# A four-layer graph network on one core: layer 0's sums turned, two of its quarters side by side, and the start of layer 1

## The chip, the core and the metric

The kernel runs on one core of one Trainium2 chip. The metric is the device time of one execution in microseconds (us), median of the runs shown. TensorE (PE) multiplies matrices, VectorE (DVE) and ScalarE (ACT) work on elements, GpSimd (POOL) takes powers, casts and issues the converting loads, and SyncE (SP) issues the other transfers. Matrix products land in eight PSUM banks, each 128 partitions by 512 float32.

## What is computed

4096 nodes with 64 features each (`x`) pass through four layers; `adj` is a 4096 x 4096 matrix of zeros and ones. Each layer normalizes `x`, takes the positive part `h`, and adds a graph operation to `x`:

```python
# layer 0: of each row's ones, the last 100 count, weighted by halves from the end
rank = jnp.cumsum(mask, axis=1); deg = rank[:, -1:]; k = jnp.minimum(deg, 100.0)
w = mask * jnp.where(rank - (deg - k) > 0, 0.5 ** (k - (rank - (deg - k))), 0.0)
x = x + w @ (h @ weight) + bias
# layer 1: attention between linked nodes; q, k and h come from small linear steps
att = adj * sigmoid((2 + 2 * (qm @ k.T)) / att_scale + att_bias)
support = att @ h;  x = x + support / norm(support)
# layer 2: two gated steps, each with adj @ (...);  layer 3: adj @ (66 columns), then an output map
```

## The kernel before

**Tiles.** `adj` stands in memory turned (`adjT`, sources by targets, float32). The targets are cut into four quarters q of 1024 and the sources into 32 blocks b of 128, so there are 128 blocks (q, b) of 128 x 1024. All 128 stay in SBUF as one byte per element, in the tiles `A` (two blocks in one tile). Nothing is loaded twice for the layers: layers 1 to 3 read `A`.

**Layer 0** (`stream0`, called once for each quarter, blocks from 31 down to 0). 113 blocks are loaded by a DMA that POOL issues and that converts float32 to bytes (`dma` at L1025). One such load waits until the load eight before it has landed (`after=loads[-8:-7]`). The other 15 (`staged`) are loaded as float32 by SP, cast by POOL (L1210) and tested on DVE (L1187), which looks for values other than 0 and 1. The byte pairs are read as float16, two elements in one number. For each half c of a block, PE adds a product with the triangular matrix `tri` (`ftri` in the profile) into a PSUM bank, which then holds each place's count of later ones in a coded form. `weigh` on ACT (L1233) or DVE (L1235) turns the count into the weight 2^-count, in 128 x 512 pieces. Then a product with `upd` (`fupd`) turns the bank into the start of the next block. So tri, weigh, upd, tri is a chain through all the blocks of a quarter, one for each half. `add` multiplies the weights as stationary operand (four 128 x 128 pieces) with `S0`, the layer's input in two float16 parts of 64 columns, into `sums`.

**After a quarter** `post0` reduces the sums on DVE (two reductions at L990), turns them with four transposes (L1038), multiplies with `w0` and adds to `X[q]`. `pre1` then computes that quarter's share of layer 1: `S1`, the keys `kT` and the queries, with four powers on POOL (`root`, L997), four turns and three linear steps on PE, and a number of DVE and ACT steps. The queries go out to memory and back in another order (`qs`).

**Layer 1** (`stream1`) goes by quarters, and in each by 16 pairs of blocks. A pair takes two scores on PE (four products of a 64 x 64 corner of the array each), a sigmoid on ACT (L1008, `fatt_mul`), a product with `A` on DVE (L968) and two adds on PE. Pair i needs `kT[i // 4]`. Scores take two neighbouring PSUM banks out of banks 0 to 3, and the accumulator takes two out of 4 to 7.

**What sets the order.** `Plan.order` writes each engine's instructions in one fixed order, made from planned costs, priorities and free PSUM banks and SBUF tiles. On the chip each engine goes through its list in order. So an instruction that waits holds all behind it. On POOL the powers, the casts and the issue of loads share one list. Layer 1's scores have a lower priority than all of layer 0. The 113 blocks not tested in layer 0 are tested later, in layers 1 and 2. `load_x` and `load_consts` bring the four quarters of `x` and the weights in between the first blocks (`gate`, L1683).

In the scheduled order of before, three scores stand ahead of the last `tri` product of quarter 3, and the rest behind it.

Of the kernel before, what the change touches and what calls it, by code (L numbers as in the profile page):

```python
# [38 lines left out]
def general_kernel(ctx: ExitStack, tc: tile.TileContext, t: dict, out: bass.AP):  # L39
# [11 lines left out]
    adjT = t["adjT"]  # L51
    N = adjT.shape[0]
    NB = N // P
# [163 lines left out]
    def aggregate(m, lhs, weigh, descending, evac, post):  # L217
# [8 lines left out]
        for h in range(NH):  # L226
# [16 lines left out]
            for i, pair in enumerate(pairs):  # L243
                a = adjp.tile([P, 2, HN], F32, tag="a", name="a")
                nc.sync.dma_start(a, adjT[pair * 2 * P:(pair + 1) * 2 * P, h * HN:(h + 1) * HN]
                                  .rearrange("(j p) n -> p j n", p=P))
                for s in range(NCH // 2):
                    rhs = weigh(h, i, pair, s, a)
                    if behind is not None:
                        accumulate(*behind)  # L250
                    behind = (i, pair, s, rhs)
                if h > 0 and i == 1:
                    post(h - 1)
# [380 lines left out]
class Plan:  # L634
# [7 lines left out]
    TABLE = 1.28  # L642
    RATE = 0.42e6
    LAND = 2.0

    def __init__(self, nsb, limits, anywhere):
        self.ops = []
        self.nsb = nsb
        self.limits = limits
        self.anywhere = anywhere  # L650
        self.clock = 0.0

# [43 lines left out]
    def find(self, b):  # L696
# [20 lines left out]
        if self.psn.get(b.kind, 0) + b.units > self.limits.get(b.kind, 8):  # L717
            return math.inf, None
        places = range(0, 4, 2) if b.units == 2 else range(8) if b.kind in self.anywhere else range(4, 8)
        if b.kind != "nw" and self.psn.get("single", 0) >= 3:  # L720
# [180 lines left out]
def fast_kernel(ctx: ExitStack, tc: tile.TileContext, t: dict, out: bass.AP, flag: bass.AP):  # L901
    nc = tc.nc
    adjT = t["adjT"]
    N = adjT.shape[0]
    NB = N // P
# [8 lines left out]

    plan = Plan(NSB, {"cnt": 2, "sum": 2, "sc": 4, "acc": 3, "acc2": 3, "acc3": 6, "nw": 4,
                      "w": (24, 16), "g": (5, 6), "stage": (5, 8), "qd": (4, 0), "mx": (4, 0)}, ("sum", "acc3"))

# [229 lines left out]

    loads = []

# [27 lines left out]
    def staged(q, b):  # L1177
        n = q * NB + NB - 1 - b
        return n > 8 and n % 8 == 1

# [12 lines left out]
    def later_test(b, q, after, cost):  # L1193
        s = sb(4, "stage")
        dma(s, View(None, lambda: adjT[b * P:(b + 1) * P, q * 2 * CW:(q + 1) * 2 * CW]), P * 2 * CW * 5, 8.0, after=after)
        return test(b, q, s, 9.0, cost)


    def stream0(q, behind):
        cnt = [bank("cnt") for _ in range(2)]  # L1200
        sums = [bank("sum") for _ in range(2)]
        for b in range(NB)[::-1]:
            a = a8(q, b)
            src = View(None, lambda b=b: adjT[b * P:(b + 1) * P, q * 2 * CW:(q + 1) * 2 * CW])
            if b in behind:
                behind[b](loads[-1:], (q, b + 1))
            if staged(q, b):
                s = sb(4, "stage")
                dma(s, src, P * 2 * CW * 5, 1.0, after=loads[-2:-1])
                plan.op({"POOL": 1.4}, lambda e, a=a, s=s: G_.tensor_copy(a.get().bitcast(U8), s.get(), saturate=False),  # L1210
                        (s,), (a,), 1.0)
                test(b, q, s, 1.9, {"DVE": 1.58})
            else:
                loads.append(dma(a.bits(U8), src, P * 2 * CW * 4, 0.9 if len(loads) < 2 else 1.0, "POOL", after=loads[-8:-7]))
            wts = []
            for c in (0, 1):
                pairs = slice(c * CW // 2, (c + 1) * CW // 2)

                def count(e, c=c, a=a, pairs=pairs, b=b, wt=tri):
                    mm(cnt[c].get()[:, :CW // 2], wt, a.get().bitcast(F16)[:, pairs], False, b == 0)  # L1220

                if b == NB - 1:
                    plan.op({"PE": 0.12}, lambda e, c=c: mm(cnt[c].get()[:, :CW // 2], mean16, half16, True, False),
                            (triv,), (cnt[c],), 1.0, "full")
                plan.op({"PE": 0.112}, count, (a, triv), (cnt[c],), 1.0, "full")
                wt = sb(1, "w").bits(I16)
                wts.append(wt)

                def weigh(e, c=c, wt=wt):
                    o = wt.get().rearrange("p (n k) -> p n k", k=2)  # L1230
                    s = cnt[c].get()[:, :CW // 2].bitcast(I8).rearrange("p (n k) -> p n k", k=4)[:, :, :2]
                    if e == "ACT":
                        S_.activation(o, s, AF.Relu, scale=-128.0)  # L1233
                    else:
                        V.tensor_scalar(o, s, -128.0, 0.0, op0=ALU.mult, op1=ALU.max)  # L1235
                plan.op({"ACT": 0.6, "DVE": 0.69}, weigh, (cnt[c],), (wt,), 0.5)
                if b:
                    plan.op({"PE": 0.112}, lambda e, count=count: count(e, wt=upd), (a, triv), (cnt[c],), 1.0, "full")
            for c in (0, 1):
                def add(e, b=b, c=c, wt=wts[c]):  # L1240
                    s = S0[b // QB].get()[:, b % QB]
                    o = sums[c].get().rearrange("p (k n) -> p k n", k=4)
                    for d in range(4):
                        mm(o[:, d, :].rearrange("p (k d) -> p k d", d=D), wt.get()[:, d * P:(d + 1) * P].bitcast(BF16), s,
                           b == NB - 1 and d == 0, b == 0)
                plan.op({"PE": 0.24}, add, (wts[c], S0[b // QB]), (sums[c],), 2.0, "full")
        return sums

    def post0(q, sums, prio):
        g = nodes("agg")  # L1250
        for c in range(2):
            red(g.part(c)[:, c * CB:(c + 1) * CB, :], sums[c].re("p (b k d) -> p b d k", k=2, d=D), CW, prio)
        fm = sb(2, "aggT")
        copy(fm, turn4(flat(g), prio), prio=prio, scale=W0 / HALF)
        tt(X[q], X[q], blocks(linear4(fm, w("w0"), prio)), ALU.add, prio=prio)
        pre1(q, prio)
# [77 lines left out]
    ends = {}  # L1334
    scores = []

    def stream1(q):
        qd = []
        for c in range(2):
# [5 lines left out]
            qd.append(v)  # L1345
        acc = [bank("acc") for _ in range(2)]
        for i in range(NB // 2):
            gs = []
            for c in range(2):
                ps = bank("sc", 2)  # L1350

                def score(e, i=i, c=c, ps=ps):
                    kb = kT[i // 4].get()[:, (i % 4) * P:(i % 4 + 1) * P]
                    o = ps.get().rearrange("p (j n) -> p j n", j=2)
                    for h in range(2):
                        for j in range(2):
                            half = slice(j * D, (j + 1) * D)
                            mm(o[h * D:(h + 1) * D, j, :], kb[half, h * D:(h + 1) * D], qd[c].get()[half, :])
                scores.append(plan.op({"PE": 0.856}, score, (kT[i // 4], qd[c]), (ps,), 3.0, "corner", after=scores[-1:]))
                g = sb(4, "g")  # L1360
                fn(g, ps, AF.Sigmoid, 1280, 1.0, "sig", View(attv.buf, lambda: att_add), View(attv.buf, lambda: att_mul))
                g3 = g.re("p (j n) -> p j n", j=2)
                m = g.re("p (k n) -> p k n", n=P)
                tt(m, m, A[q][i].bits(U8).re("p j (k c n) -> p c (j k) n", c=2, n=P)[:, c], ALU.mult, 2 * CW, 1.0)
                gs.append(g3)
            for j in range(2):
                def add(e, i=i, j=j, gs=gs):
                    b = 2 * i + j
                    s = S1[b // QB].get()[:, b % QB, :]
                    for r in range(2):  # L1370
                        half = slice(r * D, (r + 1) * D)
                        for c in range(2):
                            mm(acc[r].get()[c * D:(c + 1) * D, :], s[half, :], gs[c].get()[half, j, :], b == 0, b == NB - 1)
                ends[1, q, i] = plan.op({"PE": 0.856}, add, (*gs, S1[(2 * i) // QB]), tuple(acc), 3.1, "corner")
        return acc

    def post1(q, acc, prio):
        a = sb(2, "a")
        fn(a, acc[0], AF.Copy, prio=prio)
        tt(a, a, acc[1], ALU.add, prio=prio)  # L1380
        sup = blocks(turn4(a, prio))
# [309 lines left out]
    def load_consts(after, behind):  # L1691
        gate(Wv, lambda: W[:1, :1], behind)
        dma(Wv, View(None, lambda: t["consts"][:, :L.at["scales"].stop]), P * L.at["scales"].stop * 4, 0.1, after=after)
        for q in range(NQ):
# [4 lines left out]
    load_x(3)  # L1699
    behind = {NB - 2: lambda *a: load_x(2, *a), NB - 5: lambda *a: load_x(1, *a), NB - 9: lambda *a: load_x(0, *a),  # L1700
              NB - 13: load_consts}
    sums = {}
    for q in range(NQ):
        sums[q] = stream0(q, behind if q == 0 else {})
        post0(q, sums[q], 0.9 if q < NQ - 1 else 0.4)
    acc = {}
# [46 lines left out]
    return plan  # L1753


def pack_consts(given):
# [84 lines left out]
```

## Time and profile before

| what | value |
|---|---|
| median of the runs, lowest, highest | 689.85, 689.84, 690.35 us |
| the profiled execution, and its span | 691.17, 689.3 us |
| granted TensorE clock, mean | 0.976 |
| busy PE, DVE, ACT, POOL | 622.3, 548.6, 450.6, 167.9 us |
| last `tri` product | 202.2 us after the span's start |
| converting loads | 113 of 128 KB landed each, 9.9 us to landing (median) |
| float32 block loads by SP | 128 of 512 KB, 5.7 us to landing (median) |
| in `x_pm` loads, weights | 4 of 256 KB, 1 of 456.5 KB |

"Busy" PE includes the time in which a product runs through the array with the next one already started, so it can stand near 100% with room left. The rate in GB/s counts the bytes that land: of a converting load these are a quarter of what is read. Times in the views are microseconds from the span's start, and "x" is the number of instructions.

### The profile page before, as it was taken

The page shows a single profiled execution, that of the slowest core. Times are in us where ns is not written, and L with a number is a line of the kernel's source. Part 1 is how long each engine was busy: PE and PEld are TensorE (multiplying, and loading weights), DVE is VectorE, ACT ScalarE, POOL GpSimd, SP SyncE. Part 2 cuts the span into 40 slices and gives each one's busy share as a digit, 9 for nine tenths or more (in the row PEclk, how much of TensorE's full clock was granted, in tenths as well). Part 3 has the DMA queues.
Part 4 walks back from the last instruction along what each step waited for, and adds up shares of the span by engine and source line. Part 5 has one row for each costly group of instructions (what it writes and reads, how often), then busy time and mean ns, then how long its engine had stood idle before and what let it go on. Part 6 is the DMA issues. An engine that isn't in the chain of part 4 may idle for free.

```text
span 689.3 us, 14988 instructions
## 1 busy us (share of the span) xinstructions
PE 622.3 (90%) x6060; PEld 355.2 (52%) x6060; DVE 548.6 (80%) x1030; ACT 450.6 (65%) x680; POOL 167.9 (24%) x188
## 2 busy tenths in 40 slices
PE   4788889899999999999999999999999999999950
PEld 2666668678764443333333333344444444599950
DVE  5675776776768899998987799887988988985585
ACT  3464757577666666676665567645987698984463
POOL 6535564574422200200110010011000022202141
PEclk9899999999999999999999999999999999999995
DMA  9999989989902233422322231369689978420001
GB/s 99 181 251 106 95 66 147 178 73 157 125 17 62 77 93 97 120 62 93 108 57 97 92 112 62 123 220 390 202 264 352 342 250 260 154 63 2 3 31 36
DMA packets 39934, 91.64 MB, mean 133 GB/s; under 512 B 4656, under 2 KB 19632, under 8 KB 39856
## 3 DMA queue, kind: packets, MB, share of 16 engines
q1 hardware_dynamic: 23584, 75.78, 33.1%
q0 software_dynamic: 16272, 14.82, 24.2%
q8 instruction: 49, 0.80, 0.5%
q14 instruction: 29, 0.24, 0.1%
HBM read 130.82 MB, written 2.10 MB: 193 GB/s over the span
## 4 chain that ended last, share of the span: by engine, by line
PE 63%; DVE 16%; DMA 8%; ACT 6%; issue 3%; POOL 3%; SPq 0%; POOLq 0%; ACTq 0%; DVEq 0%
PE p L1029 61%; DVE m L968 4%; DMA A<-in_adjT 3%; ACT m L1008 3%; PE p L1038 3%; DMA m<-in_adjT 3%; DVE m L1235 2%; DVE m L985 2%; POOL s L997 2%; DMA m<-in_x_pm 2%; ACT m L1233 2%; DVE s L990 2%; DVE junk L1187 2%; POOL A L1025 1%; DVE s L968 1%
## 5 line engine op out<-in xcount | busy, mean ns | idle before, releaser
L1029 PE MATMUL p<-m,m 64*64 64x512 f32 (+1 forms) x3012 | 337.8, 476 | 8.5 <-ACT m L1008 3.7
L997 POOL TENSOR_TENSOR s<-s,powers 128x8 f32<-128x8 f32 (+1 forms) x45 | 89.3, 1992 | 461.4 <-DVE s L979 199.4
L1008 ACT ACTIVATE m<-p,fatt_add,fatt_mul 128x1024 f32<-128x1024 f32 x128 | 149.6, 1201 | 77.2 <-PE p L1029 63.6
L1029 PEld LDWEIGHTS <-m 128*128 128x128 bf16 (+1 forms) x2048 | 134.0, 105 | 75.5 <-issue 22.0
L968 DVE TENSOR_TENSOR m<-m,A 128x1024 f32<-128x1024 f32 x128 | 152.8, 1221 | 19.8 <-ACT m L1008 19.4
L1029 PEld LDWEIGHTS p<-m,m 64*64 64x64 f32 (+1 forms) x2040 | 81.0, 132 | 142.4 <-issue 81.8
L1233 ACT ACTIVATE m<-p 128x512 int16<-128x512 int8 x180 | 103.7, 596 | 52.5 <-PE p L1029 47.1
L1187 DVE SCALAR_TENSOR_TENSOR junk<-m 128x1024 uint8<-128x1024 f32 x98 | 119.5, 1220 | 8.2 <-DMA m<-in_adjT 7.3
L1029 PE MATMUL p<-A,m 128*64 128x512 fp8e4 x1024 | 116.4, 381 | 0.0
L1029 PE MATMUL p<-A,fupd 128*128 128x256 f16 x248 | 67.6, 283 | 13.9 <-DVE m L1235 6.0
L1235 DVE TENSOR_SCALAR m<-p 128x512 int16<-128x512 int8 x76 | 52.3, 690 | 30.7 <-PE p L1029 23.3
L1029 PE MATMUL p<-A,ftri 128*128 128x256 f16 x256 | 68.9, 286 | 6.5 <-POOL A L1210 3.8
L1008 ACT ACTIVATE m<-m 128x512 f32<-128x512 f32 (+4 forms) x96 | 53.6, 567 | 30.4 <-DVE m L968 14.6
L1025 POOL DMA_DIRECT2D A<-in_adjT x113 | 61.0, 553 | 39.7 <-DMA A<-in_adjT 38.4
L1029 PE MATMUL p<-m,A 128*128 128x132 f16 x1024 | 61.4, 220 | 1.5 <-ACT m L1008 1.2
L1029 PEld LDWEIGHTS <-A 128*128 128x128 fp8e4 x1024 | 60.1, 96 | 4.0 <-issue 4.0
L990 DVE TENSOR_REDUCE s<-m 128x8 f32<-128x512 f32 (+2 forms) x66 | 43.3, 661 | 9.1 <-DMA m<-in_x_pm 7.1
L1029 PEld LDWEIGHTS <-ftri 128*128 128x128 bf16 x256 | 25.6, 100 | 33.5 <-issue 26.1
L1008 ACT ACTIVATE m<-p 128x512 f32<-128x512 f32 (+4 forms) x40 | 19.2, 491 | 33.4 <-PE p L1029 24.0
L1190 ACT ACTIVATE junk<-m,big 128x1024 uint8<-128x1024 f32 x30 | 34.5, 1149 | 1.0
L1189 ACT ACTIVATE junk<-m 128x1024 uint8<-128x1024 f32 x30 | 31.4, 1047 | 1.7 <-DMA m<-in_adjT 1.5
L1038 PE MATMUL p<-fident,m 128*128 128x128 f32 x160 | 25.8, 284 | 6.8 <-DVE m L968 4.5
(102 smaller groups left out, 429.3 us busy)
## 6 DMA issues: line engine op xcount, KB each, us to landing
m<-in_adjT SPq DMA_DIRECT2D x128, 512.0 KB, 5.7
A<-in_adjT POOLq DMA_DIRECT2D x113, 128.0 KB, 9.9
m<-qs SPq DMA_DIRECT2D x16, 128.0 KB, 4.4
m<-m SPq DMA_DIRECT2D x16, 128.0 KB, 6.9
m<-in_x_pm SPq DMA_DIRECT2D x4, 256.0 KB, 6.6
qs<-m SPq DMA_DIRECT2D x4, 256.0 KB, 5.2
out_x<-m SPq DMA_DIRECT2D x3, 256.0 KB, 2.1
m<-in_consts SPq DMA_DIRECT2D x2, 256.0 KB, 5.2
```

What stands on the lines that cost most here:

```text
L968: return plan.op(cost or {"DVE": dve(n)}, lambda e: ENG[e].tensor_tensor(o.get(), a.get(), b.get(), op), (a, b), (o,), prio)
L990: return plan.op({"DVE": dve(n)}, lambda e: V.tensor_reduce(o.get(), a.get(), AX.X, ALU.add), (a,), (o,), prio)
L997: lambda e: G_.tensor_tensor(o.get(), a.get(), POWER[power].get().to_broadcast([P, n]), ALU.pow),
L1008: S_.activation(o.get(), a.get(), func, **k)
L1025: return plan.op({eng: 0.06 if eng == "SP" else 0.55}, lambda e: ENG[e].dma_start(o.get(), a.get()), (a,), (o,), prio, nbytes=nbytes, afte ...
L1029: nc.tensor.matmul(o, lhsT, rhs, start=start, stop=stop, skip_group_check=True)
L1038: nc.tensor.transpose(o[:, j * P:(j + 1) * P], s[:, j * P:(j + 1) * P], ident)
L1187: V.scalar_tensor_tensor(junk, s.get(), 0.0, s.get(), op0=ALU.not_equal, op1=ALU.not_equal, accum_out=odd[:, i:i + 1])
L1189: S_.activation(junk2, s.get(), AF.Exp, scale=-BIG0, accum_out=zeros[:, i:i + 1])
L1190: S_.activation(junk2, s.get(), AF.Exp, bias=big1, scale=BIG1, accum_out=ones_of[:, i:i + 1])
L1233: S_.activation(o, s, AF.Relu, scale=-128.0)
L1235: V.tensor_scalar(o, s, -128.0, 0.0, op0=ALU.mult, op1=ALU.max)
```

## The change

- `adj` comes in another layout: quarter, pair of blocks, source within the block, block of the pair, target. A pair of one quarter is one piece of memory. Most converting loads bring a pair at once. Each waits for the load 12 before it (`AHEAD`), where it was 8. The blocks that are staged are others (`n % 8 == 5`), the same number.
- `stream0` takes a group of quarters: quarter 0, then 1 and 2 in turns, then 3. In the group of two, each quarter has one count bank 512 wide and `weigh` works on 128 x 1024; alone, a quarter has two of 256 as before.
- `tri`, `upd` and the preset are used in two halves of 64 columns ("narrow").
- In `add` the stationary operand is `S0`, 64 columns at a time, and the weights stream past. The sums come out turned, in one bank. `post0` has no reductions and no turn.
- In layer 1 of quarter 0 the accumulator is one bank, and may lie beside the sums in banks 2 and 3. From pair 4 on, the second score of a pair lies in two single banks, and its sigmoid is two instructions of 128 x 512.

In the scheduled order of after, six scores stand ahead of quarter 3's last `tri` product; they lie after block turns 37 to 47 of the 64 of quarters 1 and 2. All of `post0` and `pre1` of quarters 1 and 2 stand among quarter 3's blocks, and those of quarter 3 behind them.

```diff
-    def stream0(q, behind):
-        cnt = [bank("cnt") for _ in range(2)]
-        sums = [bank("sum") for _ in range(2)]
+    def stream0(qs, behind):
+        cnts = {q: [bank("cnt") for _ in range(2 // len(qs))] for q in qs}
+        sums_ = {q: bank("sum") for q in qs}
...
+            dma(s, src, P * 2 * CW * 4, 1.0, after=loads[-4:-3])
...
-                loads.append(dma(a.bits(U8), src, P * 2 * CW * 4, 0.9 if len(loads) < 2 else 1.0, "POOL", after=loads[-8:-7]))
+        elif staged(q, b ^ 1) or b // 2 == NB // 2 - 1:
+            loads.append(dma(a.bits(U8), src, P * 2 * CW * 4, 0.9 if len(loads) < 2 else 1.0, "POOL", after=loads[-AHEAD:1 - AHEAD]))
+        elif b % 2:
+            loads.append(dma(A[q][b // 2].re("p j n -> p (j n)").bits(U8),
+                             View(None, lambda: adjT[q, b // 2].rearrange("p j n -> p (j n)")),
+                             2 * P * 2 * CW * 3.95, 1.0, "POOL", after=loads[-AHEAD:1 - AHEAD]))
...
-                    mm(cnt[c].get()[:, :CW // 2], wt, a.get().bitcast(F16)[:, pairs], False, b == 0)
+                for h in (0, 1):
+                    half = slice(h * D, (h + 1) * D)
+                    if parts == 1:
+                        mm(cnt[c].get()[half, :], wt[:, half], s, False, b == 0)
+                    else:
+                        mm(cnt[c].get()[half, :wide].rearrange("p (j n) -> p j n", n=D), wt[:, half],
+                           s.rearrange("p (j c n) -> p c j n", c=2, n=D)[:, c], False, b == 0)
...
-                    for d in range(4):
-                        mm(o[:, d, :].rearrange("p (k d) -> p k d", d=D), wt.get()[:, d * P:(d + 1) * P].bitcast(BF16), s,
-                           b == NB - 1 and d == 0, b == 0)
+            for k in (0, 1):
+                for c in (0, 1):
+                    mm(sums.get()[c * D:(c + 1) * D, :].rearrange("p (j n) -> p j n", n=P), s[:, k, :], v[c],
+                       b == NB - 1 and k == 0, b == 0 and k == 1)
...
     def post0(q, sums, prio):
-        g = nodes("agg")
-        for c in range(2):
-            red(g.part(c)[:, c * CB:(c + 1) * CB, :], sums[c].re("p (b k d) -> p b d k", k=2, d=D), CW, prio)
         fm = sb(2, "aggT")
-        copy(fm, turn4(flat(g), prio), prio=prio, scale=W0 / HALF)
+        copy(fm, sums, prio=prio, scale=W0 / HALF)
...
+    EARLY, APART = 1, 4
+    GROUPS = ((0,), (1, 2), (3,))
...
+        acc = [bank("acc1")] if early else [bank("acc") for _ in range(2)]
...
+                apart = early and c and i >= APART
+                ps = [bank("s1") for _ in range(2)] if apart else [bank("sc", 2)]
...
-        "x": given("x"), "adjT": transposed("adj"),
+        "x": given("x"), "adjT": given("adj").reshape(NQ, 2 * CW, -1, 2, P).transpose(0, 2, 4, 3, 1),
```

## The prediction

> **What bounds the kernel now.** The page puts PE on 63% of the chain that ended last, so I first asked where PE has room. The busy time by stretches answers, cut at the quarters of layer 0. Columns: stretch, length, then busy us (instructions) of PE, PE's weight loads, DVE, ACT and POOL, granted clock, DMA share, GB/s landed.
>
> ```profile
> 0.00:61.30 61.30, 42.56 (x377) 32.96 (x378) 36.93 (x82) 30.71 (x54) 32.98 (x54) 0.92 1.05 166
> 61.30:109.40 48.10, 41.11 (x430) 33.67 (x429) 36.23 (x65) 30.69 (x56) 28.46 (x41) 1.00 1.00 89
> 109.40:156.90 47.50, 43.06 (x436) 34.54 (x435) 35.27 (x64) 31.56 (x56) 27.91 (x36) 0.96 1.02 133
> 156.90:202.50 45.60, 42.61 (x452) 34.85 (x450) 32.87 (x61) 32.20 (x59) 18.85 (x22) 1.00 0.80 110
> 202.50:250.00 47.50, 46.64 (x405) 21.32 (x405) 40.02 (x61) 28.82 (x32) 9.19 (x4) 1.00 0.25 74
> ```
>
> Layer 0 takes 202 of 689 us, its DMA share is near 1, and DVE and ACT together are about 70% busy. From 202 to about 640 PE is the bound (20.0 of 20 us in most stretches), so what layer 0 gives up comes off the end. Next, whether the transfers are really at their limit: stretches with converting loads alone, then POOL's own timeline.
>
> ```profile
> 60.00:72.00 12.00, 10.51 (x115) 8.70 (x114) 8.96 (x15) 7.30 (x14) 5.35 (x9) 1.00 1.12 106
> 84.00:100.00 16.00, 14.10 (x145) 11.46 (x143) 12.46 (x26) 10.21 (x20) 9.77 (x13) 1.00 0.95 77
> 100.00:108.00 8.00, 6.13 (x64) 4.87 (x63) 4.71 (x7) 4.57 (x8) 7.20 (x12) 1.00 0.77 65
> ```
>
> ```profile
> 82.92 1.67 POOL L997 TENSOR_TENSOR s<-s,powers 128x8 f32<-128x8 f32 x1 [5.23 <-DVE m L977]
> 84.56 0.60 POOL L1025 DMA_DIRECT2D A<-in_adjT  x1
> 85.15 1.05 POOL L1210 CAST A<-m 128x1024 uint8<-128x1024 f32 x1
> 86.13 1.07 POOL L1025 DMA_DIRECT2D A<-in_adjT  x2
> ```
>
> Landed bytes are a quarter of those read, so the three stretches read 424, 308 and 260 GB/s: the share says busy, the rate says starved. The timeline shows why. A power at 82.92 waited 5.23 us for DVE, and the loads behind it in POOL's list waited too. Eight loads ahead are 8 x 524 KB, about 10 us at 412 GB/s; POOL's blocks are as long, so the queue runs dry.
>
> Last, the group rows that give the prices.
>
> ```profile
> L1233 ACT ACTIVATE m<-p 128x512 int16<-128x512 int8 x180 | 103.7, 596 | 52.5 <-PE p L1029 47.1
> L1235 DVE TENSOR_SCALAR m<-p 128x512 int16<-128x512 int8 x76 | 52.3, 690 | 30.7 <-PE p L1029 23.3
> L1187 DVE SCALAR_TENSOR_TENSOR junk<-m 128x1024 uint8<-128x1024 f32 x98 | 119.5, 1220 | 8.2 <-DMA m<-in_adjT 7.3
> L1029 PE MATMUL p<-A,m 128*64 128x512 fp8e4 x1024 | 116.4, 381 | 0.0
> L1008 ACT ACTIVATE m<-p,fatt_add,fatt_mul 128x1024 f32<-128x1024 f32 x128 | 149.6, 1201 | 77.2 <-PE p L1029 63.6
> ```
>
> **The loads.** To read: 128 blocks x 524 KB = 67.1 MB, with x and the weights 68.6 MB. At 412 GB/s (103 landed, 60 to 80 us) that is 167 us; starting near 4 us it would end at 171. It ends near 190 now (the share is 0.85 from 186 to 190, then 0), a mean of 369 GB/s. Twelve loads, mostly pairs, are about 20 blocks or 26 us of cover, more than any wait of POOL for a power in these stretches (longest 7 us, plus the power). Powers, casts and loads still share POOL's list, but a block of 10 us no longer empties the queue. I take an end at 171, at worst the old 190. A pair's 8 KB source row has no row in this trace; I give it the same rate, with 2% either way (3 us).
>
> Here a rule speaks against the change. The Trainium skill, "DMA: Bandwidth & Descriptors", section Specifications, limits a core's share of memory to about 358 GB/s. By it 68.6 MB need 192 us, the loads are at their limit already, and a deeper queue buys nothing. The first row above reads 424, so I go by the row: 167 us.
>
> **Quarters 1 and 2.** Up to 61 us I leave things as they are: DMA-fed with SP's traffic beside it. The data of 96 blocks is in at 4 + 51.8 MB / 0.412 = 130 us; the last pair's two turns and some waiting make it 136, where it is 156.9 now. Can the engines follow? DVE and ACT spent 133.7 us together in these quarters. One `pre1` moves on into quarter 3 (-17: quarter 2's 66.8 less 64 weighs at 0.62, 4 tests at 1.3 and 2 scores at 2.4). A weigh of 1024 instead of two of 512 saves a fixed part of 0.1 to 0.2 us (DVE 2 x 0.69 against the 1.22 of other 128x1024 forms), 64 x 0.13 = -8. Four more scores cost 4 x 2.42 = +10. That is 119 us on two engines, 60 of the 75 us. The chain per two blocks is about 0.4 + 1.1 + 0.3 = 1.8 us, 58 for 64 blocks. Both fit under the loads.
>
> PE: the row of 128*64 products shows 0.114 us each with 512 columns, so two 64-wide halves run together (0.227 a pair). Count, update and add are 4 such pairs, about 0.87 a block; before, starts lie 0.108 apart for 256 columns and 0.055 for an add piece, 4 x 0.108 + 8 x 0.055 = 0.87. No gain and no loss. But "TensorEngine Tiling (Array Packing)", Key Properties, has the array drained when the tiling mode changes, and now each turn or linear step between narrow counts changes it twice. By the trace such a change costs little: at 330.97 eight corner products (0.87 at full pace) are followed by turns at 331.99, so 0.15 us. Some 9 full-width steps a quarter x 2 x 0.15 = 2.7 us, 8 for three quarters. It is PE time inside a stretch set by loads and weighs; uncovered it would cost those 8.
>
> **Quarter 3.** Its loads end at 171, but two `pre1` now lie between its blocks. DVE and ACT: 65.1 now, + 16.5 for the second `pre1` without its reductions, - 1.4 for the other's reductions, - 2.4 for the score that moved: 78 us. At the present 71% of two engines this is 55 us; with more filler for the gaps of the chain I take 83%, 47 us. Bounds: 40 us (loads end) and 55. Last `tri`: 136 + 47 = 183, bounds 176 and 191, against 202.2. So 19 us.
>
> **Layer 1.** "Begun early" is small: three more scores go ahead of quarter 3, 3 x 0.87 = 2.6 us of PE taken off the bound stretch. Adds cost the same (two products of depth 128 for four of 64). Against it: 12 second scores with two sigmoids of 512 for one of 1.20. A 512-wide ACT step takes about 0.68, so +0.16 x 12 = 2 us of ACT, beside PE. And with the accumulator in banks 2 and 3, the first scores of a pair have one place, banks 0 and 1. A score then waits for the sigmoid before it (0.87 + 0.2 + 1.2 = 2.3 us), inside a pair of 3.5: covered if ACT is free. I put 1 us, bounds 0 and 6. `post0` of quarter 3 is shorter by 1.4 us of reductions and a turn; it hides beside scores. The later layers keep their work, so the shift stays to the end; the last test loads move with it.
>
> Sum: 19 + 2.6 - 1 = 21 us; rounded to 22 for the shorter `post0` where it does show. The profiled execution was 691.17 (span 689.3 and 1.9 around it), 1.3 above the median; off the median, 689.85 - 22 = 668.
>
> **The rivals.** (A) *Layer 0 follows the loads*: the second `pre1` fills only gaps, last `tri` at 174. For it: idle shares of DVE and ACT near 30%. Gain 28.5 + 2.6 = 31, time 659. (B) *Quarter 3 chokes*: 71% as now, its last casts stand behind powers of two `pre1` in POOL's list, and the one score place costs its 6. Last `tri` at 191: 11 + 2.6 - 6, time 682. For it: PE waited 3.8 us for casts even before. (C) *The loads gain nothing*, by the page's limit: only the three scores, 687. Against: 424 in the row. (D) *Slower*: the two 64-wide halves of counts and adds do not run together with two-byte operands. Then a block takes 8 x 0.213 = 1.71 us of PE; 128 blocks are 219, with the other 25 about 245 against 202: 730. It decides above (202 - 25) / 128 = 1.38 us a block. Against: the 128*64 row, with float16 weights.
>
> **How the numbers follow.** Main case 0.43 (own range 662 to 676), A 0.30, B 0.15, C 0.06, D 0.06. A measurement here tells 0.2% (1.4 us) from nothing. Faster: main, A, B and nearly half of C, 0.91; the same: rest of C, 0.03; slower: D, 0.06. The range 656 to 684 takes main, B and nearly all of A.
>
> **What would show it.** Landed rates near 103 GB/s from 60 us on, and no stretch at 65 to 80; loads over by about 171. Last `tri` at about 183, and quarter 3 at about 136. POOL still waiting for powers, without starving the loads. 64-wide counts starting in pairs, 0.11 or 0.21 apart. If loads end at 171 and the last `tri` is at 190, DVE and ACT (or casts) hold it. If the first pairs of layer 1 take over 4 us each, the score place does. Wrong outright: a rate that stays under 95.

## The result, and the profile after

The changed kernel takes 692.76 us (median of 5 runs, 690.61 to 694.31); the kernel before took 689.84 in the 5 runs beside it. The ratio is 1.0044, 95% interval 1.0020 to 1.0069: slower by 0.4%. The forecast was 668, range 656 to 684. The profiled execution took 691.70 us, span 689.8; layer 0's last `tri` product comes at 208.7 us, where it was 202.2 before and 183 in the forecast. So the whole miss lies in layer 0; from there to the end the kernel takes 481.1 us, 6.0 less than before. That rest has two parts. Layer 3's first product starts at 591.6 us, where it was 597.2 before, so there the changed kernel is ahead. Layer 3 then takes 70.8 us instead of 67.1, and what follows it 2.4 us more, which takes the lead away again.

Busy time by stretches, cut at the quarters of layer 0 as for before (stretch, length, busy us and instructions of PE, PE's weight loads, DVE, ACT, POOL, granted clock, DMA share, GB/s landed). Quarters 1 and 2 run from 62 to 158:

```profile
0.00:62.00 62.00, 38.11 (x358) 24.98 (x360) 34.40 (x78) 30.78 (x54) 27.02 (x43) 0.92 1.02 161
62.00:112.00 50.00, 43.77 (x360) 24.93 (x357) 33.36 (x55) 31.08 (x38) 22.93 (x31) 1.00 1.07 111
112.00:132.00 20.00, 13.82 (x92) 4.66 (x88) 7.48 (x8) 8.30 (x8) 4.97 (x5) 0.83 0.97 151
132.00:158.00 26.00, 23.91 (x200) 12.08 (x198) 11.11 (x14) 19.61 (x20) 11.28 (x15) 1.00 1.02 143
158.00:209.00 51.00, 49.44 (x476) 31.32 (x474) 42.24 (x93) 34.91 (x67) 19.19 (x13) 1.00 0.45 89
```

The third line is the find: 20 us in which DVE and ACT work 8 us each. The counts of seven blocks start in it, where the 50 us before it started 38 (1.3 us each). The loads are not short there or earlier; the stretches that starved before are full:

```profile
60.00:72.00 12.00, 10.07 (x98) 6.31 (x96) 6.58 (x9) 6.09 (x9) 2.60 (x5) 1.00 1.07 107
84.00:100.00 16.00, 14.74 (x116) 8.34 (x114) 11.71 (x27) 10.22 (x16) 7.62 (x9) 1.00 1.07 107
100.00:108.00 8.00, 7.46 (x66) 4.34 (x63) 6.31 (x10) 4.80 (x6) 5.77 (x9) 1.00 1.06 106
172.00:180.00 8.00, 7.79 (x71) 5.19 (x68) 6.48 (x21) 5.52 (x12) 3.42 (x2) 1.00 0.16 59
```

At 107 landed (428 GB/s read) against 77 and 65 before, and a share of 0.16 from 172: the transfers do what was forecast. What stops layer 0 stands in three timelines of the changed kernel (start, us, engine, line, instruction; in brackets the idle time before it and its releaser). PE's own list:

```profile
112.07 0.62 PE L1031 MATMUL p<-m,m 128*64 128x512 bf16 x4
112.50 0.41 PE L1031 MATMUL p<-A,ftri 128*64 128x512 f16 x2
117.90 2.98 PE L1031 MATMUL p<-m,m 64*64 64x512 f32 x8 [4.99 <-DMA m<-qs]
120.81 0.64 PE L1031 MATMUL p<-A,fupd 128*64 128x512 f16 x2
```

The eight 64*64 products are the first score of layer 1, "begun early" (its sigmoid follows at 120.94). It waits for the queries to come back from memory, and both quarters' `upd` and `tri` stand behind it for 8 us. SP's list and POOL's:

```profile
43.24 1.17 SPq L1027 DMA_DIRECT2D m<-in_adjT  x2
104.97 0.33 SPq L1027 DMA_DIRECT2D qs<-m  x1
112.40 2.43 SPq L1027 DMA_DIRECT2D m<-qs  x4
114.87 1.06 SPq L1027 DMA_DIRECT2D m<-in_adjT  x2
```

```profile
127.03 2.07 POOL L1218 CAST A<-m 128x1024 uint8<-128x1024 f32 x1 [17.13 <-DMA m<-in_adjT]
129.04 0.53 POOL L1027 DMA_DIRECT2D A<-in_adjT  x1
131.32 3.71 POOL L1027 DMA_DIRECT2D A<-in_adjT  x7
```

SP issues nothing from 44.4 to 105: the store of quarter 0's queries (`qs<-m`) is at the head of its list and waits for `pre1`, and the staged float32 loads stand behind it. They leave at 114.87, land 12 us later, and only then can POOL cast (17.13 us of waiting), with eight issues of converting loads behind the casts. The same order stood on SP in the profile of before:

```profile
102.91 0.33 SPq L1025 DMA_DIRECT2D qs<-m  x1
113.40 6.75 SPq L1025 DMA_DIRECT2D m<-in_adjT  x4
```

There PE waited 2.0 us for the cast (at 124.9). So one of the two waits could have been seen in the old profile, at a lower price. The weigh rows of the changed kernel for 1024 columns:

```profile
L1260 ACT ACTIVATE m<-p 128x1024 int16<-128x1024 int8 x47 | 47.2, 1023 | 20.4 <-PE p L1031 17.7 <-issue 1.9 <-DVE m L1262 0.6
L1262 DVE TENSOR_SCALAR m<-p 128x1024 int16<-128x1024 int8 x17 | 20.7, 1222 | 16.3 <-PE p L1031 15.7 <-issue 0.6
```

A weigh of 1024 costs 1.02 or 1.22 us, and the idle time ahead of nearly all is PE's.

### The profile page after: what moved, and what is told of

It is laid out like the page before. It is cut to its first block, busy times and chain, and to the rows that moved or that the text cites. A ratio compares the mean times of both kernels' runs of the same rounds, so it can differ in the third digit from the quotient of the medians.

```text
span 689.8 us, 14048 instructions
## 1 busy us (share of the span) xinstructions
PE 613.1 (89%) x5664; PEld 307.0 (45%) x5664; DVE 531.0 (77%) x998; ACT 450.1 (65%) x651; POOL 145.0 (21%) x143
## 4 chain that ended last, share of the span: by engine, by line
PE 65%; DMA 10%; DVE 10%; ACT 8%; issue 3%; POOL 2%; SPq 0%; POOLq 0%; ACTq 0%; DVEq 0%
PE p L1031 62%; DMA A<-in_adjT 6%; ACT m L1010 4%; DMA m<-in_adjT 3%; DVE m L970 3%; PE p L1040 3%; ACT m L1260 2%; DVE junk L1190 1%; DVE m L1262 1%; POOL s L999 1%; DMA qs<-m 1%; DVE s L992 1%; DVE m L987 1%; ACT junk L1192 1%; ACT L1010 1%
## 5 line engine op out<-in xcount | busy, mean ns | idle before, releaser
L1031 PE MATMUL p<-m,m 64*64 64x512 f32 (+2 forms) x2396 | 323.3, 557 | 9.8 <-DMA m<-qs 5.0
L1010 ACT ACTIVATE m<-p,fatt_add,fatt_mul 128x1024 f32<-128x1024 f32 (+1 forms) x140 | 153.1, 1129 | 82.2 <-PE p L1031 68.3
L1190 DVE SCALAR_TENSOR_TENSOR junk<-m 128x1024 uint8<-128x1024 f32 x98 | 121.4, 1238 | 14.6 <-DMA m<-in_adjT 13.6
L1260 ACT ACTIVATE m<-p 128x512 int16<-128x512 int8 (+1 forms) x137 | 98.8, 742 | 50.6 <-PE p L1031 46.7
L1031 PEld LDWEIGHTS <-m 128*64 128x64 f16 x1536 | 89.0, 111 | 75.2 <-issue 18.2
L1031 PE MATMUL p<-A,fupd 128*64 128x256 f16 (+1 forms) x372 | 61.8, 331 | 26.2 <-DVE m L1262 16.8
L1262 DVE TENSOR_SCALAR m<-p 128x512 int16<-128x512 int8 (+1 forms) x55 | 46.7, 853 | 27.7 <-PE p L1031 25.3
L1031 PE MATMUL p<-A,ftri 128*64 128x256 f16 (+1 forms) x384 | 62.1, 323 | 2.7 <-DMA A<-in_adjT 2.7
L1031 PEld LDWEIGHTS <-fupd 128*64 128x64 bf16 x372 | 33.7, 113 | 66.8 <-issue 56.8
L992 DVE TENSOR_REDUCE s<-m 128x8 f32<-128x512 f32 (+2 forms) x66 | 43.5, 662 | 11.5 <-DMA m<-in_x_pm 7.1
L1027 POOL DMA_DIRECT2D A<-in_adjT x68 | 36.8, 549 | 46.3 <-DMA A<-in_adjT 45.5
L1031 PEld LDWEIGHTS <-ftri 128*64 128x64 bf16 x384 | 25.9, 114 | 8.7 <-issue 5.2
```

The costliest lines, as they stand in the source:

```text
L992: return plan.op({"DVE": dve(n)}, lambda e: V.tensor_reduce(o.get(), a.get(), AX.X, ALU.add), (a,), (o,), prio)
L1010: S_.activation(o.get(), a.get(), func, **k)
L1027: return plan.op({eng: 0.06 if eng == "SP" else 0.55}, lambda e: ENG[e].dma_start(o.get(), a.get()), (a,), (o,), prio, nbytes=nbytes, afte ...
L1031: nc.tensor.matmul(o, lhsT, rhs, start=start, stop=stop, skip_group_check=True)
L1190: V.scalar_tensor_tensor(junk, s.get(), 0.0, s.get(), op0=ALU.not_equal, op1=ALU.not_equal, accum_out=odd[:, i:i + 1])
```

## The experiments

"Second quarter" is the start of the 33rd product of a sigmoid with `A` on DVE, where layer 1's second quarter begins. It and the last `tri` product are from one profiled execution each, the times are medians, and the ratios are to the kernel before.

| kernel | last `tri` | second quarter | us | ratio (95%) |
|---|---|---|---|---|
| before | 202.2 | 266.1 | 689.84 | |
| after | 208.7 | 266.6 | 692.76 | 1.0044 (1.0020 to 1.0069) |
| e1_sp_clear | 194.9 | 265.0 | 685.68 | 0.9952 (0.9931 to 0.9972) |
| e2_ahead6 | 211.1 | 265.7 | 691.25 | 1.0013 (0.9997 to 1.0029) |
| e4_loads_alone | 207.5 | 267.9 | 697.03 | 1.0089 (1.0057 to 1.0121) |
| e5_loads_sp_clear | 195.6 | 258.8 | 682.76 | 0.9901 (0.9878 to 0.9924) |
| e6_tail | 207.0 | 264.8 | 691.66 | 1.0022 (1.0008 to 1.0035) |
| e8_sp_not_early | 207.2 | 264.7 | 697.88 | 1.0126 (1.0083 to 1.0169) |
| e9_sp_one_by_one | 208.9 | 278.8 | 706.78 | 1.0249 (1.0208 to 1.0291) |
| e10_no_loads | 178.0 | 245.1 | 670.43 | one run |
| e11_no_staged | 206.4 | 266.4 | 692.86 | 1.0055 (1.0042 to 1.0068) |
| e12_scores_later | 213.9 | 282.2 | 704.36 | 1.0201 (1.0170 to 1.0231) |
| e13_none_staged_scores_later | 197.8 | 265.8 | 691.56 | 1.0036 (1.0021 to 1.0051) |
| e15_before_sp_clear | 202.7 | 266.6 | 689.81 | 1.0000 (0.9988 to 1.0011) |
| e16_sp_plan_rate | 233.8 | 301.7 | 728.79 | 1.0589 (1.0548 to 1.0630) |
| e17_before_sp_q2 | 200.4 | 260.8 | 691.77 | 1.0044 (1.0027 to 1.0062) |
| e18_loads_sp_rate | 228.5 | 294.7 | 729.91 | 1.0608 (1.0565 to 1.0652) |
| e19_loads_sp_early | 194.8 | 263.0 | 686.94 | 0.9967 (0.9949 to 0.9984) |
| e20_sp_one_by_one | 200.1 | 266.7 | 691.90 | 1.0034 (1.0018 to 1.0050) |
| e21_sp_one_not_early | 196.3 | 260.2 | 689.32 | 1.0004 (0.9990 to 1.0017) |

**The list of SP.** The first theory (S) was that the store holds the staged loads. e1 creates the store behind the last staged load of quarters 1 and 2; e2 only shortens the queue, against the rival (D) that a deep queue makes the blocks land late.

```diff
-        dma(qS[q], qT, P * CW * 4, prio)
+        if q == 0:
+            held.append(qT)
+        else:
+            dma(qS[q], qT, P * CW * 4, prio)
...
         sums = stream0(qs, behind)
+        if 1 in qs:
+            dma(qS[0], held[0], P * CW * 4, 0.9, after=stages[-1:])
```

> The changed kernel, but the store of quarter 0's queries is planned behind the last staged load of quarters 1 and 2, so that on SP's list no staged load stands behind it. Theory S (SP's list: staged loads wait behind the store, which waits for pre1 of quarter 0): the hole without tri products from 112 to 127 us goes, quarters 1 and 2 end near 140 instead of 157, last tri near 190 instead of 208.7, time 675 to 680. Theory D (a float32 load takes 12 us to land because it shares the DMA engines with twelve deep pair loads): the casts still wait, the hole only moves, last tri over 203, time 688 to 693.

```diff
-    AHEAD = 12
+    AHEAD = 6
```

> The changed kernel with six converting loads ahead in place of twelve. Theory D: the float32 loads land in 6 to 8 us, the hole shrinks by 5 us or more, last tri near 202, time 686. Theory S: the staged load is issued at 115 as before, the hole shrinks by at most 3 us, last tri 205 to 209, time 690 to 693.

e1 has no hole (the same 20 us, same columns as above; the last count of quarters 1 and 2 starts at 146.0 instead of 157.3):

```profile
112.00:132.00 20.00, 16.21 (x131) 8.43 (x128) 8.40 (x9) 11.33 (x12) 5.95 (x10) 1.00 1.07 169
```

131 products and a clock of 1.00 instead of 92 and 0.83. e2 keeps the hole (no `tri` product starts from 106.4 to 119.1), and with half the queue its float32 load of 110.8 still takes 11.5 us to land: D falls. But e1 moved two things. With its store later on SP, the plan also put the first score behind quarters 1 and 2 (its sigmoid starts at 150.1 instead of 120.9). So three kernels part the two waits.

**Two waits, one behind the other.** e11 takes the staged loads out of layer 0 (the 15 tests come later), e12 only holds back the first score (the others follow it), e13 does both (from quarter 2's block 4).

```diff
     def staged(q, b):
         n = q * NB + NB - 1 - b
-        return n > 8 and n % 8 == 5
+        return False
```

```diff
-                scores.append(plan.op(..., after=scores[-1:]))
+                scores.append(plan.op(..., after=scores[-1:] or (counts[2],)))
```

> The changed kernel with no staged block in layer 0: all 128 blocks come by converting loads, none by SP and a cast, and the 15 tests of layer 0 are made later. Theory S (the store of the queries holds the staged loads behind it on SP): no hole between 112 and 132, last tri product at 190 to 196, time 684 to 687. If casts and staged loads cost more than the hole: last tri product at 183 to 188, time 678 to 683. If 15 more tests in layers 1 to 3 are not hidden: time 3 to 5 us above these.

> The changed kernel with layer 1's first scores held back, in the plan, until the last count product of quarter 2; SP's list keeps the query store ahead of the staged loads. In the changed kernel no tri product starts from 112.5 to 122.5 us: PE's list has a score there whose reloaded queries land at 117.9 and later. Theory E (that score alone makes the hole): last tri product 10 us earlier, at 197 to 200, time 682 to 685. Theory S (the staged loads behind the store alone): no change, last tri product 207 to 210, time 691 to 693. Theory B (both, one behind the other): the hole moves to the cast at about 127, last tri product 203 to 206, time 687 to 690.

> The kernel of e11_no_staged (no staged block in layer 0) with the first scores held back until quarter 2's block 4. e11_no_staged still stood still from 105 to 115 us, with the last tri product at 206.4 and 692.9 us. Theories E and B: that hole goes, last tri product at 194 to 198, time 682 to 686. Theory S alone: as e11_no_staged, 205 to 207 and 692.

In e11, without staged loads, PE stops all the same, for the score (first line). In e12, without the early score, it stops longer, for the cast (second line):

```profile
109.95 3.63 PE L1031 MATMUL p<-m,m 64*64 64x512 f32 x8 [4.58 <-DMA m<-qs]
```

```profile
129.87 0.64 PE L1031 MATMUL p<-A,ftri 128*64 128x512 f16 x2 [10.49 <-POOL A L1218]
```

Removing one leaves the other; e13 removes both and brings the last `tri` product from 206.4 (e11) to 197.8. So S alone is refuted by e11, and theory B (both) holds for the place of the hole. Its price was wrong for e12: 213.9, not 203 to 206, and 704 us, at least 14 above what was expected. And e13's 8.6 us do not reach the end: its interval touches e11's. From the last `tri` product to the end e13 takes 491.3 us, e11 485.8. The plan orders each of these kernels anew, and this rest varies from 479 (e2) to 499 us (e18). Part of it is how much of layer 1 stands ahead of the last `tri` product: six scores in e11, three in e13. At the second quarter the two are 0.6 us apart. For the rest I can name no cause.

**The loads.** e4 has the loads of after (layout, pairs, 12 ahead, other staged blocks) with the counts, sums and layer 1 of before. e5 adds the cleared list (store behind quarter 2's staged loads). e15 and e17 clear the list in before; e15's edit left SP's order as it was (quarter 1's staged loads already stood ahead), so it tells nothing, and e17 has e5's place.

```diff
+        if q == 2:
+            dma(qS[0], held[0], P * CW * 4, 0.9, after=stages[-1:])
```

(e5 and e17, with the store of quarter 0 held as in e1; `q == 1` in e15. e4 is the file of before with the change's loads, and with `RATE`, the plan's load rate, at 0.41e6 as in after, where before has 0.42e6.)

> The kernel before with the changed loads alone: the new layout, pairs, twelve ahead, the new choice of staged blocks; counts, sums, quarters one by one and layer 1 as before. The prediction's reason (full queue alone brings layer 0 forward): last tri near 188, time 676. Theory S: the staged load of quarter 1 still stands behind the query store at 103 us, a hole of 8 us or more near 120, last tri 196 to 203, time 684 to 691.

> The kernel of e4_loads_alone (counts and sums of before, one quarter at a time, loads in pairs and twelve ahead) with quarter 0's query store put behind quarter 2's place in the plan. e4_loads_alone: last tri product 207.5, 697.0 us. If the full queue pays once SP's list is clear: last tri product at 190 to 196 and 680 to 686 us, under the time of e15_before_sp_clear. If layer 0 isn't set by the loads: last tri product at 198 to 204, 688 to 693 us.

> The kernel before with quarter 0's query store put behind the last staged load of quarter 1, as in e1_sp_clear. If what e1_sp_clear gains is only the cleared list: last tri product at 194 to 197 instead of 202, time 683 to 687. If the pair of quarters beside each other is what gains once the list is clear: last tri product at 199 to 202, time 687 to 690.

> The kernel before with quarter 0's query store created behind quarter 2's staged loads, as in e5_loads_sp_clear; the loads stay single and eight ahead. If the cleared list alone is what gains in e5_loads_sp_clear: last tri product at 194 to 198, time 682 to 686. If the loads' deeper queue gains once the list is clear: last tri product at 199 to 203, time 687 to 691.

The four corners are 689.8 (neither), 697.0 (loads), 691.8 (list) and 682.8 us (both). The two need each other: a full queue does not help while the staged blocks wait behind the store, and a cleared list gains nothing with single loads. The way in e4 leads over DVE. It has no hole of 8 us; the tests of the late staged blocks (L1190) stop DVE's list for 8.8 us in all (1.5 in e5), and PE waits 8.8 us for the weighs behind them (1.8 in e5). One such pair, DVE and PE:

```profile
115.46 1.23 DVE L1190 SCALAR_TENSOR_TENSOR junk<-m 128x1024 uint8<-128x1024 f32 x1 [3.11 <-DMA m<-in_adjT]
```

```profile
117.36 0.27 PE L1031 MATMUL p<-A,fupd 128*128 128x256 f16 x1 [2.50 <-DVE m L1244]
```

e5 is the fastest kernel of this study, 1.0% under before.

**Is it the loads or the order?** e10 leaves out the loads, casts and first tests of quarters 1 to 3, which read quarter 0's blocks: it computes something else and only its pace in layer 0 counts.

```diff
-        if staged(q, b):
+        if q:
+            pass
+        elif staged(q, b):
...
-    A = [[fixed(A8[q][i]) for i in range(NB // 2)] for q in range(NQ)]
+    A = [[fixed(A8[0][i]) for i in range(NB // 2)]] * NQ
```

> Leaves out the loads, casts and first tests of quarters 1 to 3: these quarters read quarter 0's blocks, so layer 0 from quarter 1 on has its data at hand. Only layer 0's own time is to be read. Theory L (loads and casts set the pace once SP's list is clear): quarters 1 and 2 take 0.9 to 1.0 us a block instead of 1.3, and the last tri product comes at 155 to 165. Theory C (the count chains, with the steps of pre1 among them in PE's list, set the pace): quarters 1 and 2 take 75 to 82 us as in e1_sp_clear, quarter 3 about 45 to 50, last tri product at 185 to 195.

Its stretches are quarters 1 and 2, then quarter 3; the third line is quarters 1 and 2 of e1:

```profile
61.00:126.00 65.00, 64.11 (x552) 37.30 (x551) 38.37 (x55) 47.30 (x54) 6.50 (x4) 1.00 0.04 13
126.00:178.00 52.00, 49.71 (x498) 32.27 (x498) 40.66 (x88) 37.82 (x69) 14.37 (x8) 1.00 0.03 12
```

```profile
64.00:146.00 82.00, 70.00 (x560) 38.65 (x558) 45.49 (x70) 50.23 (x56) 33.51 (x46) 1.00 1.07 147
```

From the first count of quarters 1 and 2 to their last, e10 takes 65 us (60.8 to 126.2), 1.0 a block, where e1 takes 82 (64.0 to 146.0) and the chain was forecast at 58. That is theory L's pace, but its last `tri` product (155 to 165) was wrong too, since quarter 3 takes 52 us without any load. What is left in e10 is PE itself: it is busy in 64.1 of the 65.0 us (short gaps can hide in that).

e1's quarters hold 17 us more. PE is idle for 12.0 of its 82 us; 9.8 of these end with a weigh (ACT 8.9, DVE 0.9), and none ends with a load or a cast. So no late block stops PE there, although the loads are what e10 leaves out; what PE's list has between a count and its update does not cover the weigh. e16 and e18 ask whether that is only the order that the plan makes for its planned arrivals: `RATE` is set to 0.65e6 in e1's kernel (e16) and to 0.6e6 in e5's (e18), and no transfer changes.

```diff
-    RATE = 0.41e6
+    RATE = 0.65e6
```

> The kernel of e1_sp_clear with the plan's load rate set to 0.65e6 instead of 0.41e6: no transfer changes, only the order that the plan makes. In the order of e1_sp_clear 48 of 62 updates in quarters 1 and 2 are followed at once by their own quarter's next count; here 58. Theory O (that order, made for loads that arrive just in time, sets the pace): quarters 1 and 2 end at 134 to 140 instead of 146, last tri product at 184 to 190, time 677 to 682. Theory L (the blocks do arrive just in time on the chip): last tri product at 193 to 197, time 684 to 688.

> The kernel of e5_loads_sp_clear (before's counts, sums and layer 1) with the plan's load rate at 0.6e6. Theory O: last tri product at 186 to 191 instead of 195.6, time 675 to 680. Theory L: last tri product at 194 to 198 and time within 2 us of 682.8.

Theory O fell: 729 and 730 us. Three lines of e16, of PE, DVE and POOL, show what such a plan does:

```profile
108.09 1.12 PE L1040 MATMUL p<-fident,m 128*128 128x128 f32 x4 [13.22 <-DVE m L987]
```

```profile
107.35 0.69 DVE L987 SCALAR_TENSOR_TENSOR m<-m,s 128x512 f32<-128x512 f32 x1 [14.02 <-POOL s L999]
```

```profile
105.09 0.53 POOL L1027 DMA_DIRECT2D A<-in_adjT  x1 [0.94 <-DMA A<-in_adjT]
105.64 1.68 POOL L999 TENSOR_TENSOR s<-s,powers 128x8 f32<-128x8 f32 x1
```

A power stands in POOL's list behind issues that each wait for a landing; DVE waits 14 us for it, PE's turn waits for DVE, and both count chains stand behind the turn. So loads and chain meet through the lists even where no block is late. As a cause of e1's 17 us theory O is not refuted by this, since the new plan changed POOL's list as well as PE's; no run changes PE's order alone, and what makes the 17 us stays open.

**Layer 1, counts and pair, each alone.** The edits are of two lines (e8 the first, e9 the second):

```diff
-    EARLY, APART = 1, 4
+    EARLY, APART = 0, 4
-    GROUPS = ((0,), (1, 2), (3,))
+    GROUPS = ((0,), (1,), (2,), (3,))
```

e8 is e1 with layer 1's first quarter as before; e9 is e1 with the quarters one by one. Each got a new hole, so neither tells what it was made for: in e8 no `tri` product starts from 183 to 194.3, behind turns of `pre1` that wait for DVE, and in e9 quarter 1's store takes SP's head in the same way (SP silent from 116 to 154, then POOL waits 11.1 us for a cast and PE 5.1 us).

> The kernel of e1_sp_clear with layer 1's first quarter as before (two accumulator banks, scores in pairs of banks). e1_sp_clear ends layer 0 at 194.9 us and layer 1's first quarter at 265. Theory P (the single score place costs what layer 0 gained): the scores of the stretch behind the last tri product run two at a time again, layer 1's second quarter starts near 260, and the time is 4 to 5 us below e1_sp_clear's 685.7. Rival Q (the start of layer 1 waits for the keys and queries of quarters 1 to 3, whatever the banks): second quarter within 2 us of 265, time within 1.5 us of 685.7, or above it, since the early scores are lost.

> The kernel of e1_sp_clear with the quarters 1 and 2 one behind the other. If the two count chains beside each other are worth what the prediction took them for, the last tri product moves from 194.9 to about 202 and the time goes up by 5 to 7 us (691 to 693). If the pace of layer 0 is set by the loads, the last tri product stays at 194 to 197 and the time within 2 us of 685.7.

Cleaner are e19 (e5 with after's first quarter of layer 1, `EARLY = 1`, `APART = 0`), e20 (the same layer 1 and place of the store, with after's counts and sums one quarter at a time) and e21 (e20 with `EARLY = 0`, against e5).

> The kernel of e5_loads_sp_clear with the changed kernel's first quarter of layer 1: one accumulator bank beside the sums, and all second scores of a pair in two single banks. If the single place for scores costs what e1_sp_clear lost behind layer 0: layer 1's second quarter starts at 263 to 266 instead of 258.8, time 686 to 690. If it is covered, as the prediction had it: second quarter at 258 to 261, time within 1.5 us of 682.8.

> The changed kernel with the quarters 1 and 2 one behind the other, the query store behind quarter 2's staged loads, and all second scores of layer 1's first quarter in two single banks. Differs from e19_loads_sp_early (last tri product 194.8, 686.9 us) in the narrow counts and turned sums alone. If the mode changes and halves are hidden beside the chain, as the prediction had it: last tri product at 193 to 197, time 685 to 688. If they are not: 8 us later, 201 to 205 and 693 to 696. If the pair of quarters gains (e1_sp_clear: 194.9, 685.7), this one is later than that by 5 us or more.

> As e20_sp_one_by_one, with layer 1's first quarter as before. Differs from e5_loads_sp_clear (last tri product 195.6, layer 1's second quarter at 258.8, 682.8 us) in the narrow counts and turned sums alone. If these are hidden: last tri product at 194 to 197, second quarter at 257 to 260, time 680 to 684. If not: last tri product at 201 to 205, time 688 to 691.

From e5 to e19 the second quarter moves by 4.2 us and the time by 4.2, from e21 to e20 by 6.5 and 2.6: the early form costs that. The score place is seen on ACT. In e1, with one place for all scores of the first pairs, the sigmoids (1024 wide) start 2.5 us apart, where e5 (the second two lines) has them 1.6 apart, and 2.1 the next:

```profile
197.93 1.21 ACT L1010 ACTIVATE m<-p,fatt_add,fatt_mul 128x1024 f32<-128x1024 f32 x1 [0.39 <-PE p L1031]
200.48 1.20 ACT L1010 ACTIVATE m<-p,fatt_add,fatt_mul 128x1024 f32<-128x1024 f32 x1 [0.39 <-PE p L1031]
```

```profile
198.89 1.21 ACT L1010 ACTIVATE m<-p,fatt_add,fatt_mul 128x1024 f32<-128x1024 f32 x1 [2.34 <-PE p L1031]
200.49 1.21 ACT L1010 ACTIVATE m<-p,fatt_add,fatt_mul 128x1024 f32<-128x1024 f32 x1 [0.40 <-PE p L1031]
```

From e19 to e20 the narrow counts and turned sums cost 5.0 us (last `tri` product 5.3 later), from e5 to e21 6.6 us in the median, though there the last `tri` product moves by only 0.7 (e21's profiled execution was its fastest, 3.0 us under its median). So they cost something, by a way that the traces did not settle; the place of the sums goes with them (one bank out of 2 and 3, where before has two anywhere). e1 against e20 gives the pair of quarters: 6.2 us gained, 5.2 of it at the last `tri` product (the two also differ in `APART` and in which staged loads stand ahead of the store).

**The end.** In the changed kernel layer 3 takes 70.8 us instead of 67.1. The theory was that the products of its two last units stand mixed; e6 holds the last unit back.

```diff
-                ends[4, u, s, d] = plan.op(..., 6.0, "full")
+                ends[4, u, s, d] = plan.op(..., 6.0, "full",
+                                              after=(ends[4, 6, NQ - 1, CB - 1],) if u == 7 and s == 2 else ())
```

> The changed kernel, with the last unit of layer 3 (unit 7) held until unit 6 is complete, as the order of before had it; layer 0 as in the changed kernel. Theory T (the two units taken in turns end together, and two closing chains fall behind the last product): from the last layer-3 product to the end 25 us instead of 27.6, layer 3 itself 2 to 4 us shorter, time 687 to 690. If the turns cost nothing: 692 to 693.

Layer 3 stays at 70.8 and the interval overlaps after's: nothing speaks for this theory (the trace does not tell the units apart). e1, with the same code for layer 3, takes 66.6 us there, and e5 71.4, so the length goes with the order that the plan makes. What in it does this, no run shows.

## Why the prediction was wrong

The medians make a ladder, each step with intervals apart: before 689.8; loads and cleared list together -7.1 (e5); layer 1's early start +4.2 (e19); narrow counts and turned sums +5.0 (e20); the pair of quarters -6.2 (e1); the store, and with it the first score, back where the change has them +7.1 (after). The forecast was -22 for the sum.

The intervals speak of the executions only. Each step also gives the plan a new order, and this moves what lies behind the edit. At layer 3's first product the same six kernels stand at 597.2, 584.3, 587.2, 591.6, 590.2 and 591.6 us (one profiled execution each). So the first three steps keep their sign there (-12.9, +2.9, +4.4), but the pair of quarters is worth 1.4 us and the store's place 1.4. The rest of their 6.2 and 7.1 comes mainly in layer 3, which e1 passes in 66.6 us and e20 and after in 71.2 and 70.8. That these two steps are worth what the ladder says is not shown; at the last `tri` product they are 5.2 and 13.9 us.

- **The loads.** Right as transfers: 428 GB/s read in the stretches that had starved, over by about 173 (forecast 171). The row held, and 358, the limit that the Trainium skill gives in "DMA: Bandwidth & Descriptors", Specifications, did not: that row of the page halves a stack's 716 GB/s between two cores, and here one core runs. Wrong as a cause: "the queue runs dry" was real, but e4 fills the queue and layer 0 ends at 207.5, not earlier.
- **"The last pair's two turns and some waiting make it 136."** This is the step that failed: 157.3, so 21.3 of the 25.7 us that layer 0 missed. The step took the later of two sums, the data (130) and the engines (58 to 60 us), and let each hide the other. It did not name what is queued behind the query store on SP, nor behind the early score on PE. With both waits gone (e1) 11.3 us come back; the last 10 go with PE's waits for weighs, for which only the trace speaks. PE's own work was priced by the block (0.87 us) and summed for no quarter: without loads these quarters take 65 us (e10), with PE busy in nearly all of it, where the chain was put at 58; with loads and no hole they take 82.
- **"'Begun early' is small", 2.6 us gained, 1 lost.** Also failed. The first score stands among count products and waits there for a round trip through memory; this opened the hole at 112.5. And where that is away (e19), the early form costs 4.2 us, near the upper bound of 6 for the score place.
- **Quarter 3, 47 us.** The work was right (77.2 us on DVE and ACT, forecast 78); the share was not: 76% instead of 83%, so 51 us. The lower price for the share (71%, 55 us) was too pessimistic. A share of DVE and ACT was the wrong thing to guess: PE is busy in 49.4 of these 51 us (fifth row of the first view), and in 49.7 of 52 without loads (e10).
- **"No gain and no loss" for counts and adds, mode changes 8 us if uncovered.** The halves do run together (the four products of an add take 0.43 us, 112.07 to 112.50 in PE's list above), so rival D is out by its mechanism. The working had a slip: four pairs at 0.227 are 0.91 a block; at the 0.215 measured here they are the 0.86 that it wanted. But in e20 the turned form costs 5 us that were put at nothing.
- **The later layers keep the shift.** From the last `tri` product to the end 481.1 us instead of 487.1, about 3 better than the sum had it. That the sum of this rest came out is luck: it is 12.1 us shorter up to layer 3 and 6.1 longer from there on, and in the other kernels it varied by as much, so I claim no cause.
- **The rivals.** None was what happened. The mechanism of B (casts behind waits, one score place) came nearest, but in quarters 1 and 2, and 11 us dearer than its 682; the slower end came by waits in lists, and not by PE's rate.

## What to carry to other kernels

Where a fixed list sets the order, an instruction that is moved early brings its wait with it: before pricing it, write down when its operand arrives and what stands behind it on that engine, and on each queue that feeds it. A deeper queue and a freer list can be worthless alone and worth 1% together, so a null result of one does not clear the other. And removing one of two waits that end close together shows nothing; remove both, then put one back.

## What was not expected of the hardware

After PE stood still for 5.0 us in the changed kernel, its granted clock was 0.5 for the next 4.9 us of work. The stretches are (the clock is the third column from the end):

```profile
112.90:116.00 3.10, 0.01 (x1) 0.00 (x0) 1.23 (x1) 0.42 (x1) 0.00 (x0) 1.00 1.05 104
117.90:122.80 4.90, 4.90 (x18) 1.50 (x20) 0.62 (x1) 1.20 (x1) 0.00 (x0) 0.50 1.09 193
122.80:124.60 1.80, 1.80 (x16) 0.43 (x12) 0.60 (x1) 1.44 (x2) 0.00 (x0) 0.99 1.03 209
```

A pair of `upd` products takes 0.64 us at 120.81, where it took 0.41 at full clock. So the hole cost about 2.5 us of PE (4.9 x 0.5) beyond its length. Behind the holes of e11 and e12 the clock was 0.5 for 6.7 and 4.2 us of work. The Trainium skill, "TensorE: Matmul & The Clock Gate", Part 1, gives half rate after an idle window of about 3.4 us, for about the next 3.4 us of work. The half rate agrees; the length does not, by these three figures. Nor is 3.4 us a safe length for a wait here: the 2.0 us for the cast in before was followed by a clock of 0.5 from 126.6 to 130.0, and 2.2 us in e5 by none.

A 256 KB store through SP lands in 7.3 us in the changed kernel (104.97 to 112.27), where the median of the kernel's four stores is 2.4. It is not the depth of the queue: with eight single loads ahead (before) the same store takes 7.9 us and with six pairs (e2) 7.4; without loads (e10) it takes 3.5. In e1 it takes 14.3; two float32 loads leave SP just ahead of it there (106.8 and 107.3), as in e8 (14.5). That these make the difference is argued, not shown by a run of its own.
